# A graph network's softmax: each 128x128 transposition as two of 64 rows on the two row halves of TensorE

## The chip, the cores and the metric

The kernel runs on one core of one Trainium2 chip. The metric is device time in microseconds (us) of one execution, as the median of several runs. The engines are named as in the profile: PE is TensorE's matrix multiply, PEld its weight load, DVE is VectorE, ACT is ScalarE, POOL is GpSimd, SP is SyncE. PSUM is the accumulator memory that PE writes and that DVE and ACT read[...].

## What is computed

Four graph layers, each behind a layer norm and a ReLU, and each added to its input, on x of 32 batches, 512 nodes and 64 features, all in fp32. The last two have the softmax that the change touches:

```python
x = x + L0(h, adj, ...)          # h = relu(layernorm(x)), before each layer
x = x + L1(h, adj, ...)          # two rounds of adj @ h @ w, with relu
# layer 2: graph attention
Wh = h @ W.T; e = leaky_relu(Wh @ a1 [:, None] + Wh @ a2 [None, :], 0.2)
att = softmax(where(adj > 0, e, -9e15), axis=-1)
x = x + elu(att @ Wh)
# layer 3: eight heads, then an output layer, each of the form
def gat_layer(x, graph, W, b):
    h = x @ W
    s = (h @ h.T) * graph
    a = softmax(where(s == 0, -1e16, s), axis=2)
    return a @ h + b
```

## The kernel before, in words

The 512 nodes are four blocks of 128. Layers 0 and 1 come first, in four groups of eight batches, and are not touched. Layers 2 and 3 are done in *units*, each of which is two softmax problems of 512x512 side by side: `Gat` (layer 2: two batches, 16 units), `Heads` (layer 3: two heads of one batch, 128 units) and `Out` (the output layer: two batches, 16 units). After the 16 Gat units, eight Heads units and one Out unit alternate; the Out unit of a pair of batches stands behind the third Heads unit of the second batch after it. All are subclasses of `Pair`.

A unit takes four steps of each kind, and `run` (L609) interleaves the units by hand: in one turn of the loop at L618 it issues

- `scores(r)` of the current unit: two matmuls of 64 rows each, one for each problem, on the two row halves of PE (L472, s_ps, a tile of two banks, two such tiles);
- `transpose(j)` (L332) of the unit before, five turns late: for each of the two problems, the four 128x128 blocks of the probabilities p_att (L338) into one bank of the pool ps_m (pt_ps), and a copy of the bank to SBUF on ACT (L343, pt_att);
- with `transpose(1)`, `recips` (L355): the reciprocal of the softmax sums on DVE (L357, rec), eight small matmuls that spread it (L361, rec_ps), a copy (L369, recb);
- `values(j)`, a turn later: two matmuls av (L350) with the transposed probabilities;
- `end(j)`: the product with recb on DVE (L373, o_att), for Heads the head's output (L544, y_ps, and on ACT L549, cat), for Gat and Out the way back into x (L381);
- `prep(j)` for the next unit: for Heads the layer norm on DVE (L497 to L505, hn), a transposition with its copy (L178 and L180, hx) once in a batch, and g_ps (L516); for Out the accumulation gT_ps over all heads (L567, 16 matmuls over four turns), and gV_ps (L576);
- `soft(r)` of the current unit: for Heads and Out, DVE multiplies the scores by the graph (L461, s_att), makes the mask (L465, t_att) and takes the row maxima (L322, twice); ACT takes the exponential with its sum (L326, twice, p_att).

"First step" to "fourth step" below are these turns, counted by `scores(0)` to `scores(3)`. By the lags, rec_ps and g_ps lie in the third, y_ps in the fourth.

The pool ps_m has three banks, which serve pt_ps, rec_ps, g_ps, y_ps, gT_ps, gV_ps and the others; ps_s has two tiles of two banks, ps_v one bank for av. The engines run their own queues. The order in a queue follows the order of issue only roughly: the framework that builds the program moves instructions by its own estimate of when their inputs are ready. In the built program the reciprocal of L357 stands much earlier than the loop has it: mostly just behind the first s_att of the next unit, once the last L326 of its own unit is due. And the two L549 of a Heads unit stand between the two L326 of a fourth step.

Of the kernel before, what the change touches and what calls it, by code (L numbers as in the profile page):

```python
# [8 lines left out]
F32 = mybir.dt.float32  # L9
# [5 lines left out]
P = 128  # L15
# [7 lines left out]
def gnn_stack_kernel(  # L23
# [22 lines left out]
    nc = tc.nc  # L46
    B, N, F = x.shape
    C = N // P
# [59 lines left out]
    ident = const.tile([P, P], F32, name="ident")  # L108
# [12 lines left out]
    with tc.tile_pool(name="ps_setup", bufs=2, space=PSUM) as ps:  # L121
        for k in range(C):
            pt = ps.tile([P, N], F32, name="pt")
# [139 lines left out]
    ps_m = ctx.enter_context(tc.tile_pool(name="ps_m", bufs=3, space=PSUM))  # L263
# [13 lines left out]
    pt = ps_m.tile([P, H, F], F32, name="whT_ps", tag="m")  # L277
# [24 lines left out]
    def halves(k):  # L302
        return slice(k * F, (k + 1) * F)

    class Pair:
# [26 lines left out]
        def transpose(self, j):  # L332
            pt = pbuf.tile([P, 2, N], F32, name="pt_att", bufs=3)
            self.pts = getattr(self, "pts", []) + [pt]
            for k in range(2):
                ps = ps_m.tile([P, N], F32, name="pt_ps", tag="m")
                for r in range(C):
                    nc.tensor.transpose(  # L338
                        ps[:, r * P : (r + 1) * P],
                        self.p[:, k, r, j * P : (j + 1) * P],  # L340
                        ident,
                    )
                nc.scalar.copy(pt[:, k, :], ps)  # L343

        def values(self, j):
            pt = self.pts.pop(0)
# [339 lines left out]
```

## Time and profile before

| what | us |
|---|---|
| median of 3 runs (3112.18 to 3113.51) | 3113.04 |
| the profiled execution, its own time | 3115.21 |
| its span, first to last instruction | 3113.4 |
| PE busy in the span | 2842.9 |
| DVE busy | 2436.9 |
| ACT busy | 2005.0 |
| layers 0 and 1, about | 0 to 451 |
| Gat units, about | 465 to 800 |
| Heads and Out units, about | 766 to 3107 |

How to read it: a line of the timeline gives the start, the length, the engine, the line, the operation, the tiles out<-in, the shape and the count; what stands in brackets behind it is the idle time of the engine before it, and which instruction ended that. `64*128` behind a matmul is the rows and columns of PE that it uses. An fp32 matmul shows as two instructions, a transposition as one. Matmuls are pipelined, so that the start of one to the start of the next says more than their lengths. Times are from one profiled execution, which took 2.2 us more than the median of the runs.

### The profile page before, as it was taken

The numbers are of one execution on the slowest core, as the hardware profiler recorded it, in microseconds if no ns is written. First come the engines' busy times: TensorE is split into PE (matmuls) and PEld (weight loads), VectorE is DVE, ScalarE is ACT, GpSimd is POOL, SyncE is SP. The second block draws the span as 40 slices with busy tenths as digits, with TensorE's granted clock in tenths as the row PEclk, the third lists the DMA queues.
The fourth block names the chain that finished last, engine by engine and source line by source line (L and its number), as shares of the span: only waits on it lengthen the run. The fifth ranks groups of instructions, "written<-read, shape, count | busy, mean of one in ns | idle before, by whom it ended". The sixth has DMA issues, their size and how long they took to land.

```text
span 3113.4 us, 41619 instructions
## 1 busy us (share of the span) xinstructions
PE 2842.9 (91%) x15532; PEld 1380.7 (44%) x15532; DVE 2436.9 (78%) x4802; ACT 2005.0 (64%) x4586; POOL 99.1 (3%) x49
## 2 busy tenths in 40 slices
PE   4665658788999999999999999999999999999998
PEld 2333335444444444444444444444444444444443
DVE  5335348989988888979898988888898979898884
ACT  0110106766777777777777777777777777777775
POOL 3102100000000000000000000000000000000000
PEclk9887887998999999999999999999999999999999
DMA  3000000000000000000000000000000000000000
GB/s 80 0 0 0 0 1 1 1 1 1 1 1 5 1 4 1 4 1 4 1 4 1 4 4 1 4 1 4 1 4 1 4 1 4 1 5 4 1 4 4
DMA packets 9867, 13.09 MB, mean 4 GB/s; under 512 B 968, under 2 KB 9328, under 8 KB 9536
## 3 DMA queue, kind: packets, MB, share of 16 engines
q1 hardware_dynamic: 6832, 7.34, 0.7%
q8 instruction: 122, 2.00, 0.3%
q10 hardware_dynamic: 2080, 2.10, 0.2%
q0 software_dynamic: 752, 0.99, 0.2%
q14 instruction: 81, 0.66, 0.1%
HBM read 6.23 MB, written 4.19 MB: 3 GB/s over the span
## 4 chain that ended last, share of the span: by engine, by line
PE 82%; DVE 11%; ACT 4%; issue 1%; POOL 1%; DMA 0%; POOLq 0%; ACTq 0%; DVEq 0%
PE av L350 19%; PE pt_ps L338 18%; PE s_ps L472 17%; PE nt_ps L195 6%; PE rec_ps L361 5%; PE g_ps L516 4%; PE y_ps L544 4%; PE gT_ps L567 3%; PE po L206 2%; ACT p_att L326 2%; DVE s_att L461 1%; DVE l_att L432 1%; DVE mean L140 1%; DVE hn L164 1%; DVE t_att L322 1%
## 5 line engine op out<-in xcount | busy, mean ns | idle before, releaser
L326 ACT ACTIVATE p_att<-t_att,negmax 128x512 f32<-128x512 f32 x1152 | 825.2, 717 | 465.5 <-DVE negmax L322 465.4
L461 DVE TENSOR_TENSOR s_att<-s_ps,adj_p 128x1024 f32<-128x1024 f32 x576 | 703.4, 1222 | 225.3 <-PE s_ps L472 225.3
L338 PEld LDWEIGHTS pt_ps<-ident,p_att 128*128 128x128 f32 x5120 | 553.6, 141 | 509.5 <-ACT p_att L326 186.9
L322 DVE CUSTOM_DVE_ANT_0 t_att<-s_att,t_att 128x512 f32<-128x512 f32 x1152 | 752.4, 687 | 13.4
L343 ACT COPY pt_att<-pt_ps 128x512 f32<-128x512 f32 x1280 | 679.3, 581 | 119.1 <-PE pt_ps L338 118.8
L338 PE MATMUL pt_ps<-ident,p_att 128*128 128x128 f32 x5120 | 714.2, 282 | 28.5 <-DVE e L414 12.1
L472 PE MATMUL s_ps<-hx,g 64*128 64x512 f32 x2048 | 660.1, 624 | 2.0 <-DVE s_att L461 2.0
L350 PE MATMUL av<-pt_att,hn 128*64 128x512 f32 x2048 | 579.0, 611 | 0.0
L465 DVE TENSOR_SCALAR t_att<-s_att 128x1024 f32<-128x1024 f32 x576 | 393.1, 683 | 24.7 <-ACT pt_att L343 0.9
L472 PEld LDWEIGHTS s_ps<-hx,g 64*128 64x128 f32 x2048 | 204.3, 185 | 310.9 <-issue 121.4
L326 ACT ACTIVATION_READ_ACCUMULATOR p_att<-t_att,negmax 128x1 f32 x1152 | 216.1, 188 | 0.0
L361 PE MATMUL rec_ps<-ident,rec 128*64 128x128 f32 x2560 | 185.8, 283 | 22.3 <-ACT p_att L326 19.7
L195 PE MATMUL nt_ps<-adj_t,hn 128*128 128x512 f32 x256 | 135.0, 669 | 60.5 <-DVE hn L168 60.5
L199 ACT COPY nt<-nt_ps 128x512 f32<-128x512 f32 x48 | 28.1, 586 | 237.8 <-PE nt_ps L195 237.8
L361 PEld LDWEIGHTS rec_ps<-ident,rec 128*64 128x64 f32 x2560 | 144.0, 139 | 56.2 <-issue 26.4
L549 ACT ACTIVATE cat<-y_ps,bh 128x512 f32<-128x512 f32 x256 | 159.7, 673 | 4.4 <-PE y_ps L544 4.4
L350 PEld LDWEIGHTS av<-pt_att,hn 128*64 128x64 f32 x2048 | 115.6, 135 | 76.7 <-issue 76.4
L544 PE MATMUL y_ps<-o_att,wh_sb 64*128 64x512 f32 x512 | 145.6, 641 | 1.6 <-ACT pt_att L343 0.8
L516 PE MATMUL g_ps<-hx,m 64*128 64x512 f32 x256 | 143.7, 641 | 1.1 <-ACT pt_att L343 1.0
L246 DVE SCALAR_TENSOR_TENSOR x<-po,x 128x256 f32<-128x256 f32 x32 | 12.1, 419 | 167.5 <-PE po L206 167.5
L567 PE MATMUL gT_ps<-cat,wo_sb 128*64 128x512 f32 x512 | 131.4, 595 | 0.0
L373 DVE TENSOR_TENSOR o_att<-av,recb 128x512 f32<-128x512 f32 x160 | 108.9, 681 | 23.1 <-PE av L350 21.9
(117 smaller groups left out, 2118.5 us busy)
## 6 DMA issues: line engine op xcount, KB each, us to landing
out_dram<-x SPq DMA_DIRECT2D x32, 128.0 KB, 1.8
x<-in_x_dram ACTq DMA_DIRECT2D x2, 1024.0 KB, 19.0
x<-in_x_dram SPq DMA_DIRECT2D x2, 1024.0 KB, 19.0
adj_raw<-in_adj_dram SPq DMA_DIRECT2D x1, 1024.0 KB, 5.7
wh_sb<-in_L_gnn_Wh_dram POOLq DMA_DIRECT2D x2, 256.0 KB, 8.0
wo_sb<-in_L_gnn_W_out_dram POOLq DMA_DIRECT2D x1, 256.0 KB, 8.7
wl<-in_L_gnn_net_params_dram POOLq DMA_DIRECT2D x4, 16.0 KB, 8.0
bias_b<-in_L_gnn_bias_dram POOLq DMA_DIRECT2D x1, 32.0 KB, 7.7
```

What stands on the lines that cost most here:

```text
L195: nc.tensor.matmul(p, lhsT=lhs(k), rhs=adj_t[:, k, :], start=(k == 0), stop=(k == C - 1))
L322: nc.vector.tensor_tensor_reduce(out=ns[k], in0=s[k], in1=t[k], scale=-1.0, scalar=BIG, op0=OP.add, op1=OP.min, accum_out=self.negmax[:, k ...
L326: nc.scalar.activation(self.p[:, k, r, :], ns[k], AF.Exp, bias=self.negmax[:, k, r : r + 1], scale=-1.0, accum_out=self.sum[:, k, r : r + 1],)
L338: nc.tensor.transpose(ps[:, r * P : (r + 1) * P], self.p[:, k, r, j * P : (j + 1) * P], ident,)
L343: nc.scalar.copy(pt[:, k, :], ps)
L350: nc.tensor.matmul(self.av[halves(k), :], lhsT=self.v(k, j), rhs=pt[:, k, :], start=(j == 0), stop=(j == C - 1),)
L361: nc.tensor.matmul(ps[halves(k), r * P : (r + 1) * P], lhsT=rec[:, k, r : r + 1].to_broadcast([P, F]), rhs=ident, start=True, stop=True,)
L461: nc.vector.tensor_tensor(s, ps, adj_f[:, r, None, :].to_broadcast([P, 2, N]), OP.mult)
L465: nc.vector.tensor_scalar(t, s, 0.0, FLOW_NEG, op0=OP.is_equal, op1=OP.mult)
L472: nc.tensor.matmul(u.s_ps[:, k], lhsT=g[halves(k), r * P : (r + 1) * P], rhs=x[halves(k), :], start=True, stop=True,)
L516: nc.tensor.matmul(ps, lhsT=m2[rows, 2 * i : 2 * i + 2, :].rearrange("p h f -> p (h f)"), rhs=self.x[rows, :], start=True, stop=True,)
L544: nc.tensor.matmul(ps, lhsT=wh_sb[halves(k), h, :], rhs=self.o[halves(k), :], start=True, stop=True,)
```

## The change

The two problems' eight blocks are transposed as sixteen: each 128x128 block of p_att is split into its upper and lower 64 rows, and each half is transposed on its own row half of PE, with the matching 64x64 part of the identity. The two halves alternate. All the upper halves go to one bank and all the lower halves to another, so that a bank now holds both problems instead of one. The two copies on ACT each take a bank and write it into the two problems' rows of pt_att, in runs of 64 elements. Both banks are asked for at the start.

```diff
         def transpose(self, j):
             pt = pbuf.tile([P, 2, N], F32, name="pt_att", bufs=3)
             self.pts = getattr(self, "pts", []) + [pt]
+
+            ps = [ps_m.tile([P, 2, C, F], F32, name="pt_ps", tag="m") for half in range(2)]
             for k in range(2):
-                ps = ps_m.tile([P, N], F32, name="pt_ps", tag="m")
                 for r in range(C):
-                    nc.tensor.transpose(
-                        ps[:, r * P : (r + 1) * P],
-                        self.p[:, k, r, j * P : (j + 1) * P],
-                        ident,
-                    )
-                nc.scalar.copy(pt[:, k, :], ps)
+                    for half in range(2):
+                        nc.tensor.transpose(
+                            ps[half][:, k, r],
+                            self.p[halves(half), k, r, j * P : (j + 1) * P],
+                            ident[halves(half), halves(half)],
+                        )
+            pth = pt.rearrange("p k (r half q) -> p k r half q", r=C, half=2)
+            for half in range(2):
+                nc.scalar.copy(pth[:, :, :, half, :], ps[half])
```

## The prediction, as it was put on record

> **What bounds the kernel now.** First the totals, then the stage that holds three quarters of the span, then the chain of waits, then a stretch of the timeline. The first line below is the page's busy time of each engine; the second a window over the stage with the head and output units (its columns: length, then PE, PEld, DVE, ACT, POOL busy with instruction counts, granted clock); the third the chain that ended last.
>
> ```profile
> PE 2842.9 (91%) x15532; PEld 1380.7 (44%) x15532; DVE 2436.9 (78%) x4802; ACT 2005.0 (64%) x4586; POOL 99.1 (3%) x49
> ```
>
> ```profile
> 800.00:3080.00 2280.00, 2271.13 (x12858) 1061.18 (x12855) 1935.09 (x3807) 1719.06 (x3963) 4.57 (x2) 1.00 0.01 3
> ```
>
> ```profile
> PE 82%; DVE 11%; ACT 4%; issue 1%; POOL 1%; DMA 0%; POOLq 0%; ACTq 0%; DVEq 0%
> ```
>
> In that stage PE has 9 us free of 2280; DVE is busy 85%, ACT 75%. The timeline of PE in one step (start, length, line, count):
>
> ```profile
> 2049.01 1.09 PE L338 MATMUL pt_ps<-ident,p_att 128*128 128x128 f32 x8
> 2050.04 1.08 PE L350 MATMUL av<-pt_att,hn 128*64 128x512 f32 x4
> 2051.05 1.13 PE L472 MATMUL s_ps<-hx,g 64*128 64x512 f32 x4
> 2052.11 1.09 PE L338 MATMUL pt_ps<-ident,p_att 128*128 128x128 f32 x8
> ```
>
> Start to start: transposes 1.02 us, av 1.01, s_ps 1.06, together 3.09 with no gap. A plain unit (four steps; the third adds rec_ps and g_ps, the fourth y_ps) runs from s_att at 2049.13 to the same point at 2064.08: 14.95 us. So PE sets the pace. But DVE stands close behind, and its order matters. DVE at the end of one unit and through the next:
>
> ```profile
> 2047.25 0.69 DVE L322 CUSTOM_DVE_ANT_0 t_att<-s_att,t_att 128x512 f32<-128x512 f32 x1
> 2047.86 0.69 DVE L322 CUSTOM_DVE_ANT_0 t_att<-s_att,t_att 128x512 f32<-128x512 f32 x1
> 2049.13 1.23 DVE L461 TENSOR_TENSOR s_att<-s_ps,adj_p 128x1024 f32<-128x1024 f32 x1 [0.57 <-PE s_ps L472]
> 2050.68 0.20 DVE L357 RECIPROCAL rec<-sum_att 128x8 f32<-128x8 f32 x1 [0.32 <-ACT p_att L326]
> 2052.71 1.22 DVE L461 TENSOR_TENSOR s_att<-s_ps,adj_p 128x1024 f32<-128x1024 f32 x1
> 2056.39 1.22 DVE L461 TENSOR_TENSOR s_att<-s_ps,adj_p 128x1024 f32<-128x1024 f32 x1
> 2060.12 1.22 DVE L461 TENSOR_TENSOR s_att<-s_ps,adj_p 128x1024 f32<-128x1024 f32 x1 [0.43 <-PE s_ps L472]
> ```
>
> DVE is idle 0.57+0.32+0.43 = 1.32 us in this unit. The reciprocal needs the sum that ACT makes last, and ACT puts two activations of the head output between its last two exponentials:
>
> ```profile
> 2047.98 0.72 ACT L326 ACTIVATE p_att<-t_att,negmax 128x512 f32<-128x512 f32 x1 [0.86 <-DVE negmax L322]
> 2048.70 1.25 ACT L549 ACTIVATE cat<-y_ps,bh 128x512 f32<-128x512 f32 x2
> 2049.84 0.72 ACT L326 ACTIVATE p_att<-t_att,negmax 128x512 f32<-128x512 f32 x1
> 2050.45 0.19 ACT L326 ACTIVATION_READ_ACCUMULATOR p_att<-t_att,negmax 128x1 f32 x1
> ```
>
> Exponential to reciprocal: 2047.98 to 2050.68, 2.70 us, whatever PE does. Today s_att stands ahead of the reciprocal on DVE and covers most of it. Once per nine units it doesn't (the unit ahead of an output unit), and there the trace shows the naked wait:
>
> ```profile
> 2097.72 0.69 DVE L322 CUSTOM_DVE_ANT_0 t_att<-s_att,t_att 128x512 f32<-128x512 f32 x1
> ...
> 2100.54 0.20 DVE L357 RECIPROCAL rec<-sum_att 128x8 f32<-128x8 f32 x1 [2.12 <-ACT p_att L326]
> 2102.80 1.22 DVE L461 TENSOR_TENSOR s_att<-s_ps,adj_p 128x1024 f32<-128x1024 f32 x1 [2.06 <-PE s_ps L472]
> ```
>
> Here the 2.12 us cost nothing: PE was later still.
>
> **What the Trainium skill says.** "TensorE: Matmul & The Clock Gate", Part 3: matmuls on different row groups run side by side, and the loads of weights overlap. The trace agrees: four s_ps matmuls on alternating row halves take 1.13 us, each 0.59 or more; one 512-column stream on the whole array takes 0.41 (eight nt_ps in 3.44: (3.44-0.59)/7), so four in a row would need 1.8. "TensorEngine Tiling (Array Packing)", Gotcha 1: row tiles must write different banks, which the two tiles of the change do; Key Properties: a change of tiling mode drains the array. The trace agrees: s_ps costs 1.06 between other modes and 0.96 behind y_ps, of its own mode. "PSUM — Partial Sum Buffer", Engine vs sequencer instructions: VectorE and ScalarE are strict FIFO, so what stands behind a waiting reciprocal waits too; the row at 2100.54 agrees.
>
> **The transposes on PE.** 5120 of 128x128 become 10240 of 64x128, 16 per call instead of 8. The trace has such an instruction: whT_ps, eight in a row on one row half, 64 columns each. Two answers of the timeline, cut 0.1 us apart:
>
> ```profile
> 451.32 0.37 PE L279 MATMUL whT_ps<-ident,wh_sb 64*128 64x64 f32 x3 [0.89 <-PE po L206]
> 451.32 0.49 PE L279 MATMUL whT_ps<-ident,wh_sb 64*128 64x64 f32 x5 [0.89 <-PE po L206]
> ```
>
> Two more take 0.12: 0.06 each, against 0.12 for a whole one ((1.09-0.28)/7, 282 ns being the mean of one). If the halves run in pairs, a call is 7 x 0.06 plus about 0.18 to the next mode: 0.60 instead of 1.02. If they run one after the other, 16 x 0.06 is 1.0 and nothing is gained. I take pairs, since s_ps shows them. s_ps and the transposes are then of one mode: 0.10 less. Together 0.52 per call, 2.08 per unit: PE needs 12.9 instead of 14.95.
>
> **The copies.** Still two per call of 512 elements (581 ns each); they read a bank in one run and write runs of 64. No row shows ACT writing so; 0 is taken, up to 20 ns more (below zero excluded: same elements). They can begin only when the whole call is done, 0.6 us after its start instead of 0.5 for the first: nothing, as ACT waits on DVE.
>
> **The two banks at once.** Three banks serve all small results. A call now needs two of them at its start, the second about 0.44 us earlier than today. In plain units the banks come free by the copies of the step before, ahead of need. While an output unit's gT_ps holds one, the call waits for both copies; counted below.
>
> **What moves on DVE.** The instruction order of the two built programs differs there. In the program before, 126 of 160 reciprocals stand behind the s_att of the next unit and 16 (the units with gT_ps) ahead of it. In the changed one, 18 stand behind it and 124 ahead, directly behind the second L322 of the fourth step: 7 units of 9 have changed sides. The ACT order (exponential, two cat, exponential) stays, and so does PE's. Behind the waiting reciprocal stand s_att and all of the next unit's softmax. So DVE's loop in a plain unit is: steps without idle, 3.21 (in the unit before: s_att at 2041.44, the last L322 at 2044.04, and 0.61 from one L322 to what follows), 3.68 (2052.71 to 2056.39, with o_att), 3.21 and 3.21, plus rec 0.12, plus the naked wait 2.12: 15.6 us. One more term: g_ps in the third step needs the bank whose copy ACT makes after the second step's exponentials. In the trace that copy ends 5.2 us after the second s_att (57.32+0.53 against 52.71), and the fourth step's s_att starts 2.02 after g_ps (58.10 to 60.12): 7.2 against DVE's own 3.68+3.21 = 6.9. That adds 0.3: 15.95, 1.0 more than today.
>
> **The sum**, per cycle of nine units (eight head, one output; 16 cycles):
> - seven units with cat and the moved reciprocal: 7 x 1.0 = +7.0;
> - two of them carry hn and hx: today 0.59 each on PE; then DVE pays 0.61 for the hx copy and 0.7 for hn, of which 0.3 lies in the g_ps wait: 2 x (1.0-0.59) = +0.8;
> - the unit whose fourth step has no cat keeps its reciprocal behind s_att, and loses DVE's idle: -0.4;
> - the unit with gT_ps is PE's own (23.77 from 2079.03 to 2102.80): four calls x 0.52 = 2.1, and PE enters it some 0.9 further ahead of DVE than today (the naked wait just before gives it the time), less 0.3 for banks: -2.7 (bounds -1.5 and -5).
>
> +4.7 per cycle, +75 in all. The layers before the units are untouched; the first 16 units (490 to 800) are held by DVE (277 of 310 busy) and keep their reciprocal's place: 0, bounds -15 and +10. Against the profiled execution, 3115.2 us (span 3113.4), that is 3190; the median of the runs lies 2 below it, so **3188**.
>
> **Rivals.**
> - *PE's gain comes through.* If the moved reciprocal doesn't stop DVE (its sum comes early, or the wait falls where DVE is idle anyway), a plain unit falls to DVE's 13.3 and small waits, 14.0: 8 x 0.95 + 2.7, less 1.4 for hn and hx, 9 per cycle, 2970. For it: PE is 99.6% busy now. Against: DVE is FIFO, and the 2.12 is measured. It turns at 1.3 us: if the wait is shorter than DVE's idle of today, the change is faster.
> - *The halves don't pair.* Calls stay at 1.0; the plain units don't notice (PE 14.95 is under 15.95), the gT units lose their gain: +2.7 x 16 = +43, 3230.
> - *PE cools.* PE would idle about a fifth of the time. Between 490 and 800, where PE is busy 83%, the granted clock is 0.91; if it fell so here, the gT units and g_ps stretch: some 5% of PE's 2200 us, 3300.
> - *Gains and losses cancel.* The gT unit gains 5 instead of 2.7, the g_ps wait is hidden: 4.7-2.3-2.1 = 0.3 per cycle, 3118.
>
> **How the numbers follow.** The likeliest 0.55 (its own range 3150 to 3230), PE's gain 0.13, no pairing 0.13, cooling 0.07, cancelling 0.12. About 0.2% is what a measurement of this kernel can tell from no change. Faster: 0.13 and 0.03 of the cancelling case; same: 0.05; slower: the rest, 0.79. The range from 3110 to 3265 leaves out PE's gain and most of the cooling.
>
> **What would show it.** Right: the reciprocal's idle before it grows from 71 us in total to 200 or more, released by p_att L326; s_att waits for s_ps almost only in gT units; a call of 16 takes about 0.6 us; PE's share of the chain falls and DVE's and ACT's rise. Wrong: a call still takes 1.0 (no pairing), a clock under 0.98 after 800 us (cooling), or DVE over 92% busy there with little idle before the reciprocal (the gain came through).

## The result and the profile after

The changed kernel takes 3201.45 us (median of 4 runs, 3199.8 to 3202.94), the kernel before beside it 3113.28 us (3112.18 to 3115.0): a ratio of 1.028, 95% interval 1.0265 to 1.030. The execution profiled has a span of 3200.1 us. Code lines from L345 on stand four lower than before: L340 are the transpositions, L347 the copies, L361 the reciprocal, L465 s_att, L476 s_ps, L520 g_ps, L548 y_ps, L553 cat. In the runs further down the same instructions stand at other lines again; go by the names of the tiles.

First the page's busy times of the changed kernel, then the window over the Heads and Out units, then the chain that ended last:

```profile
PE 2642.8 (83%) x20652; PEld 1339.2 (42%) x20652; DVE 2432.6 (76%) x4802; ACT 2002.8 (63%) x4586; POOL 99.0 (3%) x49
```

```profile
800.00:3080.00 2280.00, 2007.75 (x16775) 985.40 (x16775) 1875.31 (x3697) 1659.05 (x3833) 4.57 (x2) 1.00 0.01 3
```

```profile
DVE 48%; PE 27%; ACT 20%; issue 4%; POOL 1%; DMA 0%; POOLq 0%; DVEq 0%; ACTq 0%
```

PE lost 200 us of work. In the window it was busy 2271 of 2280 us, and now is 2008; its share of the chain fell from 82% to 27%. But no engine took its place: DVE is busy 1875 us in the window, less than the 1935 of before. When the bound engine gets faster, the time gets longer and every engine is busy for less of it, the chain must run through waits from one engine to another. PE's granted clock is 1.00 as before, so it did not cool.

Four groups of the page of the changed kernel (line, tiles, count; busy us, mean ns; idle time before them and who ended it):

```profile
L465 DVE TENSOR_TENSOR s_att<-s_ps,adj_p 128x1024 f32<-128x1024 f32 x576 | 697.6, 1211 | 114.8 <-PE s_ps L476 114.7
...
L347 ACT COPY pt_att<-pt_ps 128x512 f32<-128x512 f32 x1280 | 679.8, 580 | 89.2 <-PE pt_ps L340 87.8
...
L520 PE MATMUL g_ps<-hx,m 64*128 64x512 f32 x256 | 143.7, 641 | 139.7 <-ACT pt_att L347 139.7
L361 DVE RECIPROCAL rec<-sum_att 128x8 f32<-128x8 f32 x160 | 32.2, 201 | 266.8 <-ACT p_att L326 266.8
```

Before, s_att waited 225 us for s_ps and the reciprocal 71 us for the last exponential. Now s_att waits 115, the reciprocal 267: DVE waits for ACT more than for PE. The timeline of DVE through a plain unit of the changed kernel, from one reciprocal to the next:

```profile
2067.44 0.20 DVE L361 RECIPROCAL rec<-sum_att 128x8 f32<-128x8 f32 x1 [2.12 <-ACT p_att L326]
2067.56 1.17 DVE L465 TENSOR_TENSOR s_att<-s_ps,adj_p 128x1024 f32<-128x1024 f32 x1
...
2070.72 1.22 DVE L465 TENSOR_TENSOR s_att<-s_ps,adj_p 128x1024 f32<-128x1024 f32 x1
...
2074.41 1.22 DVE L465 TENSOR_TENSOR s_att<-s_ps,adj_p 128x1024 f32<-128x1024 f32 x1
...
2077.98 1.22 DVE L465 TENSOR_TENSOR s_att<-s_ps,adj_p 128x1024 f32<-128x1024 f32 x1 [0.27 <-PE s_ps L476]
...
2083.47 0.20 DVE L361 RECIPROCAL rec<-sum_att 128x8 f32<-128x8 f32 x1 [2.12 <-ACT p_att L326]
2083.59 1.17 DVE L465 TENSOR_TENSOR s_att<-s_ps,adj_p 128x1024 f32<-128x1024 f32 x1
```

16.03 us from one s_att at the head of a unit to the next, against 14.95 before. And PE in one step of the changed kernel:

```profile
2144.74 1.13 PE L476 MATMUL s_ps<-hx,g 64*128 64x512 f32 x4
2145.70 0.66 PE L340 MATMUL pt_ps<-ident,p_att 64*128 64x64 f32 x16
2146.30 1.08 PE L354 MATMUL av<-pt_att,hn 128*64 128x512 f32 x4
```

The call of sixteen halves takes 0.60 us to the next start, against 1.02 for eight whole ones, and s_ps 0.96 against 1.06. The change does on PE what it says.

For what follows, the starts of s_att (four to a unit) cut the trace into units. The lengths of the nine units of a cycle, as medians over ten cycles (us), for both kernels and for the five experiments that the argument needs:

| unit | before | after | run 2 | run 1 | run 3 | run 9 | run 12 |
|---|---|---|---|---|---|---|---|
| 1, ahead of gT, with hn | 14.95 | 16.28 | 16.29 | 15.18 | 14.73 | 14.65 | 14.16 |
| 2, with gT_ps | 23.77 | 21.13 | 22.04 | 22.89 | 22.90 | 22.29 | 22.52 |
| 3, the Out unit | 14.94 | 16.08 | 16.60 | 14.16 | 14.24 | 14.23 | 13.75 |
| 4, with hx | 15.54 | 16.63 | 16.64 | 15.36 | 15.04 | 14.83 | 14.34 |
| 5, no cat at its end | 14.28 | 13.71 | 13.71 | 14.38 | 13.94 | 13.83 | 13.47 |
| 6, with hn and back_ps | 15.35 | 16.93 | 17.02 | 15.17 | 15.25 | 15.24 | 14.75 |
| 7, plain | 14.95 | 16.02 | 16.03 | 14.61 | 14.24 | 14.24 | 13.75 |
| 8, with hx | 15.54 | 16.64 | 16.64 | 15.37 | 15.04 | 14.83 | 14.34 |
| 9, plain | 14.95 | 16.02 | 16.03 | 14.79 | 14.33 | 14.23 | 13.75 |
| sum (16 cycles) | 144.3 | 149.5 | 151.0 | 141.9 | 139.7 | 138.4 | 134.8 |
| first s_att of a Heads unit, at | 765.8 | 767.2 | 758.4 | 764.2 | 765.6 | 765.1 | 765.0 |

### The profile page after: what moved, and what is told of

Read it like the earlier page. It is cut to its first block, busy times and chain, and to the rows that moved or that the text cites. A ratio compares the mean times of both kernels' runs of the same rounds, so it can differ in the third digit from the quotient of the medians.

```text
span 3200.1 us, 51783 instructions
## 1 busy us (share of the span) xinstructions
PE 2642.8 (83%) x20652; PEld 1339.2 (42%) x20652; DVE 2432.6 (76%) x4802; ACT 2002.8 (63%) x4586; POOL 99.0 (3%) x49
## 3 DMA queue, kind: packets, MB, share of 16 engines
q8 instruction: 161, 2.64, 0.4%
## 4 chain that ended last, share of the span: by engine, by line
DVE 48%; PE 27%; ACT 20%; issue 4%; POOL 1%; DMA 0%; POOLq 0%; DVEq 0%; ACTq 0%
DVE s_att L465 15%; DVE t_att L322 12%; ACT p_att L326 12%; DVE t_att L469 9%; PE nt_ps L195 6%; PE s_ps L476 4%; ACT cat L553 4%; PE g_ps L520 3%; PE av L354 3%; PE gT_ps L571 3%; DVE o_att L377 2%; ACT pt_att L347 2%; PE po L206 2%; PE pt_ps L340 2%; DVE hn L164 1%
## 5 line engine op out<-in xcount | busy, mean ns | idle before, releaser
L465 DVE TENSOR_TENSOR s_att<-s_ps,adj_p 128x1024 f32<-128x1024 f32 x576 | 697.6, 1211 | 114.8 <-PE s_ps L476 114.7
L322 DVE CUSTOM_DVE_ANT_0 t_att<-s_att,t_att 128x512 f32<-128x512 f32 x1152 | 752.6, 687 | 13.5
L347 ACT COPY pt_att<-pt_ps 128x512 f32<-128x512 f32 x1280 | 679.8, 580 | 89.2 <-PE pt_ps L340 87.8
L340 PE MATMUL pt_ps<-ident,p_att 64*128 64x64 f32 x10240 | 588.2, 228 | 165.8 <-ACT pt_att L347 74.5
L340 PEld LDWEIGHTS pt_ps<-ident,p_att 64*128 64x128 f32 x10240 | 486.9, 139 | 551.0 <-issue 181.1
L476 PE MATMUL s_ps<-hx,g 64*128 64x512 f32 x2048 | 704.6, 625 | 6.5 <-DVE s_att L465 6.5
L476 PEld LDWEIGHTS s_ps<-hx,g 64*128 64x128 f32 x2048 | 240.8, 186 | 286.4 <-issue 73.2
L520 PE MATMUL g_ps<-hx,m 64*128 64x512 f32 x256 | 143.7, 641 | 139.7 <-ACT pt_att L347 139.7
L361 DVE RECIPROCAL rec<-sum_att 128x8 f32<-128x8 f32 x160 | 32.2, 201 | 266.8 <-ACT p_att L326 266.8
L548 PE MATMUL y_ps<-o_att,wh_sb 64*128 64x512 f32 x512 | 193.9, 643 | 0.9 <-DVE o_att L377 0.9
L553 ACT ACTIVATE cat<-y_ps,bh 128x512 f32<-128x512 f32 x256 | 159.8, 673 | 6.6 <-PE y_ps L548 6.6
L520 PEld LDWEIGHTS g_ps<-hx,m 64*128 64x128 f32 x256 | 37.7, 184 | 253.0 <-ACT pt_att L347 250.7
```

Of the source, the lines that this page charges most:

```text
L322: nc.vector.tensor_tensor_reduce(out=ns[k], in0=s[k], in1=t[k], scale=-1.0, scalar=BIG, op0=OP.add, op1=OP.min, accum_out=self.negmax[:, k ...
L340: nc.tensor.transpose(ps[half][:, k, r], self.p[halves(half), k, r, j * P : (j + 1) * P], ident[halves(half), halves(half)],)
L347: nc.scalar.copy(pth[:, :, :, half, :], ps[half])
L465: nc.vector.tensor_tensor(s, ps, adj_f[:, r, None, :].to_broadcast([P, 2, N]), OP.mult)
L476: nc.tensor.matmul(u.s_ps[:, k], lhsT=g[halves(k), r * P : (r + 1) * P], rhs=x[halves(k), :], start=True, stop=True,)
L520: nc.tensor.matmul(ps, lhsT=m2[rows, 2 * i : 2 * i + 2, :].rearrange("p h f -> p (h f)"), rhs=self.x[rows, :], start=True, stop=True,)
```

## The experiments

All of them change only the order on an engine, or the order of the halves. A line of order is given by

```python
def behind(later, earlier):     # later comes after earlier in its engine's queue; no wait is added
    tc.add_manual_dep(later.ins, earlier.ins.name,
        mybir.DependencyInfo(mybir.DependencyClass.NoSync, mybir.DependencyReason.DATA), reason="order")
```

`satt` lists the s_att instructions and `exps` the exponentials, in the order of issue. Times are medians against the kernel before on the same chip (3112.4 to 3113.1 us).

Theory A is the prediction's: the reciprocal, moved ahead of s_att, makes DVE wait for ACT with nothing beside it. Theory B is its rival: the two banks that a call now needs at once hold up g_ps and s_att. (A bank is what one of the kernel's PSUM tiles of 128x512 fp32 values takes; ps_m hands out three.)

### Runs 1 to 4: the reciprocal's place, with halves and without

Run 1 keeps the change and puts the reciprocal back behind the first s_att of the next unit:

```diff
-            nc.vector.reciprocal(rec, self.sum)
+            done = nc.vector.reciprocal(rec, self.sum)
+            behind(done, satt[-2])
```

> The halves stay as in the changed kernel; only the reciprocal stands again behind the first s_att of the next unit, where the kernel before has it. Theory A (the moved reciprocal, which waits 2.12 us and holds up s_att, is what costs): its idle falls to about 1.0 us per unit, since s_att and its 1.2 us lie in it; a plain unit 14.6 to 14.9 us instead of 16.03, PE's gain in the gT units stays: about 4.2 per cycle under the kernel before, 3046 us (3020 to 3090). Theory B (the two banks asked for at once, and the copies that end later, hold up g_ps and through it s_att): the order matters little, 3180 to 3200 us, and the plain unit stays at about 16.

Measured: 3082.2 us, ratio 0.990 (0.9885 to 0.9915). The plain unit is 14.61, as A has it, and the reciprocal waits 62 us in all instead of 267. B falls as the main cause. But 36 us of what A expected are missing, most of them in the gT unit: 22.89, not the 21.1 that the changed kernel has (1.8 x 16 = 28).

Run 2 has the kernel before, with the reciprocal alone moved to where the change has it (made at the end of its own unit, and s_att behind it):

```diff
+        def early(self):
+            self.rec = tiny.tile([P, 2, C], F32, name="rec")
+            self.done = nc.vector.reciprocal(self.rec, self.sum)
...
+                if r == 0 and last and len(satt) > n and not isinstance(units[max(u - 3, 0)], Out):
+                    behind(satt[-1], last.done)
```

> The kernel before, with whole 128x128 transpositions, and only the reciprocal moved ahead of the next unit's s_att, as it stands in the changed kernel. Theory A: the naked wait of about 2.1 us appears here too, in seven units of nine; a plain unit is at least 15.6 us, no gain in the gT units: 3185 to 3215 us. Theory B (banks and copies): no loss without the halves, 3110 to 3120 us.

Measured: 3213.1 us, ratio 1.032 (1.0305 to 1.034). Not one transposition is touched, and the kernel loses more than by the change. DVE's timeline in run 2, the head of one unit and of the next:

```profile
2021.47 0.20 DVE L366 RECIPROCAL rec<-sum_att 128x8 f32<-128x8 f32 x1 [2.12 <-ACT p_att L335]
2021.59 1.17 DVE L473 TENSOR_TENSOR s_att<-s_ps,adj_p 128x1024 f32<-128x1024 f32 x1
...
2032.61 1.23 DVE L473 TENSOR_TENSOR s_att<-s_ps,adj_p 128x1024 f32<-128x1024 f32 x1 [0.28 <-PE s_ps L484]
...
2038.11 0.20 DVE L366 RECIPROCAL rec<-sum_att 128x8 f32<-128x8 f32 x1 [2.12 <-ACT p_att L335]
2038.23 1.17 DVE L473 TENSOR_TENSOR s_att<-s_ps,adj_p 128x1024 f32<-128x1024 f32 x1
```

The same 2.12 us. The short wait of the fourth s_att for s_ps, 0.27 us in the changed kernel, stands here too, with whole blocks. The units' table shows the same lengths as after, up to 0.1 us, but for units 2 and 3. The loss is in the cycles: 6.7 x 16 = 107 us; the Gat units, whose reciprocals this run moves too, give 7 back.

Run 3 keeps the change and puts the reciprocal behind the second s_att, `behind(done, satt[-1])`; run 4 does that to the kernel before.

> The halves stay; the reciprocal stands behind the second s_att of the next unit, nearer to where its result is first needed (rec_ps in the third step). Theory A: the sum is then ready before DVE gets there, no naked wait, and a plain unit is DVE's own 13.3 plus small waits, 13.6 to 14.2: 2950 to 2995 us, the rival of the prediction in which PE's gain comes through. Theory B (banks and copies): g_ps still waits for its bank, a plain unit of about 15.5 or more, 3150 to 3200 us.

> The kernel before, whole transpositions, with the reciprocal behind the second s_att as in the third run. Theory A, in full: without the halves PE sets the pace (14.95 us per plain unit, PE busy 99% after 800 us), so DVE's relief gives nothing: 3105 to 3120 us, and what the third run gains is PE's time from the halves. If the gain came from the reciprocal's place alone, this run would be as fast as the third: below 3050 us.

Measured: 3046.0 us, ratio 0.979 (0.977 to 0.980), and 3114.3 us, ratio 1.0003 (0.999 to 1.001). Run 4 is as A expects: without the halves DVE's relief is worth nothing, since PE sets the pace. Run 3 is faster, but it misses A's 2950 to 2995. Its plain unit is 14.24 us where DVE needs 13.43. DVE's timeline of run 3, one unit:

```profile
2013.56 1.22 DVE L476 TENSOR_TENSOR s_att<-s_ps,adj_p 128x1024 f32<-128x1024 f32 x1
2014.70 0.19 DVE L370 RECIPROCAL rec<-sum_att 128x8 f32<-128x8 f32 x1
...
2020.81 1.23 DVE L476 TENSOR_TENSOR s_att<-s_ps,adj_p 128x1024 f32<-128x1024 f32 x1 [0.27 <-PE s_ps L487]
...
2024.51 1.22 DVE L476 TENSOR_TENSOR s_att<-s_ps,adj_p 128x1024 f32<-128x1024 f32 x1 [0.33 <-PE s_ps L487]
```

The reciprocal waits for nothing now. What is left are two waits for s_ps, though PE has time to spare. Runs 9 to 12 look for their cause.

The runs that vary only this and the two kernels give one table (us):

| reciprocal of the unit before | whole blocks | halves | halves give |
|---|---|---|---|
| ahead of s_att | 3213 (run 2) | 3201 (after) | -12 |
| behind the first s_att | 3113 (before) | 3082 (run 1) | -31 |
| behind the second s_att | 3114 (run 4) | 3046 (run 3) | -68 |

The halves help in every row. (In the first row about 9 us of their gain are hidden, since run 2 moves the reciprocals of the Gat units too and is faster there; in the cycles alone the halves give 24 us.) The change moved one place right and one row up.

### Run 5: what the naked wait is made of

The reciprocal is held ahead of s_att as in run 2; beside that only the two cat move behind the last exponential: `behind(cat, exps[-1])`.

> The changed kernel with its reciprocal ahead of s_att, and only the two cat activations put behind the second exponential of the fourth step instead of between the two. Theory A (the naked wait is 2.12 us because two cat of 0.57 each stand ahead of the last exponential): the reciprocal's wait falls to about 1.0 us, and with it the plain unit by up to 1.1 us from 16.03: 3075 to 3120 us. A part may come back: the next transposition needs the bank that the first cat empties, and that now ends about 0.7 us later; by the timeline of the third run, s_att could then start some 0.8 us behind the reciprocal and the plain unit be about 15.0. Rival (the wait is the latency of the exponential and its sum, whatever lies between): the wait stays at 2.1 and the time at 3195 to 3205 us.

Measured: 3110.6 us, ratio 0.9992 (0.9985 to 0.9998). The reciprocal's wait is 0.97 us in the timeline and the plain unit 15.01, both as expected. So the 2.12 us were 0.97 of exponential and sum, and two cat. Over a cycle this run takes 144.37 us, the kernel before 144.26: with a wait of 0.97 us the change just breaks even. That is a rough mark, since the later cat costs something of its own: the transpositions wait 133 us on PE for its bank from 800 to 3000 us, against 56 in the changed kernel. The Gat units, whose reciprocals this run moves too, are 8 us shorter (757.8 against 765.8), and about 4 come back behind the cycles measured.

### Runs 6 and 7: do the halves pair?

All upper halves first, then all lower ones, in run 6 on top of run 3, in run 7 on the changed kernel:

```diff
-            for k in range(2):
-                for r in range(C):
-                    for half in range(2):
+            for half in range(2):
+                for k in range(2):
+                    for r in range(C):
```

> The third run (3046 us) with one thing more: the upper halves of a call are all transposed first, then all the lower ones, instead of alternately. If the short call comes from pairs on the two row halves, a call goes from 0.58 back to about 1.0 us, PE sets the pace again with a plain unit of 14.5 to 15 us, and the time is 3090 to 3120 us. If a half costs less by itself, with or without a partner, the call stays at 0.6 and the time at 3040 to 3055 us.

> The changed kernel with the reciprocal where the change has it, and the halves in turn instead of alternately: the prediction's rival in which the halves don't pair. It put +43 us on that (gT units only). The trace of after and the second run (whole transpositions in the same order, 3213 us) say less: 22.04 against 21.13 us in the gT unit and nearly the same in the others. So 3205 to 3225 us by the runs, 3244 us by the prediction's term.

Measured: 3073.5 us, ratio 0.987 (0.986 to 0.989), and 3221.6 us, ratio 1.0345 (1.033 to 1.036). PE in run 6:

```profile
2005.58 1.13 PE L487 MATMUL s_ps<-hx,g 64*128 64x512 f32 x4
2006.54 0.96 PE L349 MATMUL pt_ps<-ident,p_att 64*128 64x64 f32 x16
2007.43 1.08 PE L363 MATMUL av<-pt_att,hn 128*64 128x512 f32 x4
```

In turn a call takes 0.89 us, alternately 0.59. Cut the timeline of PE inside one call, and the count shows how many halves have started by then. First the changed kernel, cut at 2145.80 and 2145.92, then run 6, cut at 2006.62, 2006.74 and 2006.98:

```profile
2145.70 0.29 PE L340 MATMUL pt_ps<-ident,p_att 64*128 64x64 f32 x4
2145.70 0.41 PE L340 MATMUL pt_ps<-ident,p_att 64*128 64x64 f32 x8
```

```profile
2006.54 0.28 PE L349 MATMUL pt_ps<-ident,p_att 64*128 64x64 f32 x2
2006.54 0.40 PE L349 MATMUL pt_ps<-ident,p_att 64*128 64x64 f32 x4
2006.54 0.65 PE L349 MATMUL pt_ps<-ident,p_att 64*128 64x64 f32 x11
```

Alternately, four more halves take 0.12 us: two start nearly together every 0.06 us, eight times in a call. In turn, two more take 0.12 us, each alone; then seven more take 0.25, because near the middle of the call three pairs form, presumably where the last upper and the first lower halves meet. The starts show these three pairs in 394 of the 395 calls of run 6 that ran through without a wait after 800 us. So the halves do pair, and a half alone costs the 0.06 us of whT_ps. (The two halves also write two banks; no run tells the row half from the bank.) Run 6 is no test of a call without any pair: it has 13 starts 0.06 us apart where 16 were expected. That is why its call is shorter than the 1.0 assumed, and why run 6 lies between what its two theories expect. With s_ps still at 0.96, PE is then no longer what holds a plain unit (14.23). Run 7 came out as the runs before it had let expect. Of run 6's 27 us over run 3, 16 are in the cycles (140.7 against 139.7), 12 in the units before them; of run 7's 20 over the changed kernel, 8 and 12. Why the first units lose 12 us by it was not tried.

### Run 8: one cat behind the last exponential

On top of run 3, the second cat of a unit is put behind the last exponential.

> The third run (halves alternately, reciprocal behind the second s_att, 3046 us) with the second cat of a unit put behind the last exponential; the first stays between the two, since its bank is the one that the next transposition waits for. Nothing waits for the second cat soon. If ACT's order at the end of a unit still costs anything, it shows in the gT unit, whose last step is a chain over ACT (exponential, two cat, exponential, gT copy: 7.75 us in every kernel so far): 0.6 us less there, and 3030 to 3040 us in all. If not, 3046 us as before.

Measured: 3046.0 us, ratio 0.9785 (0.977 to 0.980): nothing. The gT unit's last step stays at 7.75 us. The edit changed the order inside the chain and not its length: the gT copy still stands behind both cat and both exponentials.

### Runs 9 to 12: where the rest of PE's gain went

All four are run 3 with another order on ACT. Run 9 puts the cat ahead of the first exponential of the fourth step (`cats` holds the cat issued last, the second of the two):

```diff
+                if k == 0 and r == C - 1 and cats:
+                    behind(exps[-1], cats.pop())
```

> Where does the rest of PE's gain go? The third run (3046 us) is at 14.24 us in a plain unit, against 13.43 that DVE needs (3 x 3.21, 3.68 and 0.12). In its trace s_att waits about 0.4 us at the head of a unit: s_ps stands on PE behind a call of halves that waits for its second bank until the first cat is done, and ACT does that cat behind the first exponential of the fourth step. Here both cat stand ahead of that exponential. Theory C (the banks, of which a call needs two at once, take back a part of the gain): the fourth step loses 0.3 to 0.45 us in some seven units of nine, 2995 to 3015 us. Rival (s_ps is late for PE's own work): 3040 to 3050 us.

Measured: 3023.0 us, ratio 0.971 (0.970 to 0.973), between what the two theories expect. PE's waits from 800 to 3000 us, run 3 and then run 9 (us in all, times, longest):

```profile
PE g_ps L531 <- ACT pt_att L356: 72.2, 123, 1.2
PE pt_ps L349 <- ACT cat L564: 61.4, 111, 1.5
```

```profile
PE g_ps L535 <- ACT pt_att L360: 131.7, 124, 1.2
...
PE pt_ps L353 <- ACT cat L568: 1.2, 2, 0.7
```

The wait for cat is gone, and the wait of g_ps grew by as much. The plain unit stays at 14.24; the gain is mostly in the gT unit (22.90 to 22.29) and the two with hx. So the wait for cat was not what held the plain unit, and the expectation named the wrong bank for it.

Runs 10 and 11 put the second call's copies ahead of the second step's exponentials, without and with run 9's edit:

```diff
             for half in range(2):
-                nc.scalar.copy(pth[:, :, :, half, :], ps[half])
+                done = nc.scalar.copy(pth[:, :, :, half, :], ps[half])
+            if j == 1 and last[0] is not self:
+                behind(exps[-2], done)
```

> The third run (3046 us) with the two copies of the second call put ahead of the second step's exponentials on ACT, which in that trace is idle 1.3 us before them. g_ps waits for the bank that the first of these copies empties (0.49 us in a plain unit), and s_att of the fourth step for s_ps behind it (0.29 us). Theory C (banks): that wait goes, 0.3 us in the third step of six units of nine, 3010 to 3025 us. Rival: g_ps is late for another reason (hx, or PE's order), 3040 to 3050 us.

> Both edits to ACT's order on top of the third run. Theory C: both waits for banks go, and a plain unit comes down to about 13.5 us, DVE's own time: 2960 to 2990 us, near the 2970 of the rival in which PE's gain comes through. If the two waits stand in for each other, it is no better than the better of the two runs before.

Measured: 3056.0 us, ratio 0.982 (0.980 to 0.983), and 3043.8 us, ratio 0.978 (0.976 to 0.979). Both are slower than what they build on. ACT in run 10 shows that the edit missed its aim:

```profile
2009.61 0.72 ACT L338 ACTIVATE p_att<-t_att,negmax 128x512 f32<-128x512 f32 x1 [1.91 <-DVE negmax L334]
...
2010.33 1.05 ACT L362 COPY pt_att<-pt_ps 128x512 f32<-128x512 f32 x2
2011.28 0.73 ACT L338 ACTIVATE p_att<-t_att,negmax 128x512 f32<-128x512 f32 x1
```

The step's other exponential went ahead of the copies, after ACT had been idle for 1.91 us. g_ps still waited (78 us in all from 800 to 3000 us), and ACT was late for the fourth step, which went from 3.70 to 4.05 us. Run 12 names both, on top of run 11:

```diff
                 behind(exps[-2], done)
+                behind(exps[-1], done)
```

> In the two runs before, only one of the second step's two exponentials stood behind the copies: the trace shows the other one still ahead of them (exponential, two copies, exponential), so that g_ps still waited, 78 and 122 us in all. Here both stand behind the copies, and the two cat ahead of the fourth step's first exponential as in the ninth run (3023 us), where g_ps waits 1.03 us in a plain unit and s_att behind it 0.27 in the third and, by PE's later start, 0.32 in the fourth step. Theory C (the bank for g_ps is what is left): g_ps starts right behind av, both waits of s_att go, a plain unit takes 13.5 to 13.7 instead of 14.24 us, in six units of nine: 2955 to 2985 us. Rival (PE's own work or DVE's order makes s_ps late): 3015 to 3030 us.

Measured: 2969.0 us, ratio 0.954 (0.952 to 0.9555). PE in run 12, third step, and the window over its Heads and Out units:

```profile
2041.51 1.03 PE L372 MATMUL av<-pt_att,gV 128*64 128x512 f32 x4
2042.47 0.69 PE L540 MATMUL g_ps<-hx,m 64*128 64x512 f32 x1
```

```profile
800.00:2900.00 2100.00, 2067.26 (x17132) 1017.38 (x17130) 1902.90 (x3780) 1689.61 (x3919) 4.57 (x2) 1.00 0.01 3
```

g_ps starts 0.96 us behind av, without a wait; the wait of s_att in the third step is gone, and the plain unit is 13.75, a little above the 13.5 to 13.7 expected. What its last 0.3 us over DVE's 13.43 are was not tried. PE is busy 98% again. So Theory C holds with g_ps's bank as its place: the order in which ACT empties the three banks held back PE's gain.

That a call takes two of them at once is not shown to be the reason. The wait of g_ps is there without the halves; run 2, PE from 800 to 3000 us:

```profile
PE g_ps L528 <- ACT pt_att L352: 89.0, 87, 1.1
```

Only the wait for cat comes with the halves: 56 us on PE in the changed kernel and 61 in run 3, none in the kernel before and in run 2. The two banks can explain that one, but no run gives the halves their banks one after the other. The kernel before was not tried with run 12's order on ACT.

## Why the prediction came out as it did, step by step

The forecast was 3188 us by +4.7 us per cycle; the measured difference is 88 us, of which the cycles show 5.2 x 16 = 83.

- **PE's call.** Forecast 0.60 us, 0.10 less for s_ps; measured 0.59 and 0.10, and in the way that was forecast: eight pairs, each as long as the one half of whT_ps. The price read from whT_ps held.
- **The copies.** Taken as 0; 580 ns against 581.
- **The moved reciprocal.** Right, and shown: the 2.12 us stand in the timeline, run 2 has the loss without the change, runs 1 and 3 have the change without the loss. Forecast +1.0 per plain unit, measured +1.07. The closeness is in part luck: the forecast's terms add up to 15.85 us (15.55 and 0.3) and not to the 15.95 written, which would have been +4.0 per cycle and 3177 us; and the fourth step, 5.45 us by these terms (3.21, 0.12 and 2.12), took 5.61. That VectorE is a strict FIFO (the Trainium skill, "PSUM — Partial Sum Buffer", Engine vs sequencer instructions) is what makes one short reciprocal hold up a whole unit; in the trace s_att starts 0.12 us behind it each time. (The row at 2100.54 that the prediction named for this can't show it, since the s_att behind it waited for PE anyway.) Why the framework moved it isn't shown by any run.
- **hn and hx.** The sum was right (+0.8; measured excess over plain units +0.9), the place wrong: the units with hx lose no more than plain ones (+1.09, +1.10), those with hn do (+1.33, +1.58).
- **The unit without cat at its end.** -0.4 forecast, -0.57 measured.
- **The gT unit.** -2.7 forecast, -2.64 measured: luck, out of two wrong sizes. Forecast were 2.1 from four shorter calls, 0.9 from PE's lead, and 0.3 back for banks. Run 2, with whole blocks, has -1.73 from the lead alone: the step ahead of the unit lasts so long by the naked wait that PE is ahead when the unit starts (its first step 3.16 us instead of 4.84). The calls then give 0.91, in the second and third steps only. The last step is 7.75 us with and without halves: it is a chain from DVE over exponential, two cat, exponential, gT copy and gV_ps to s_ps, where PE waits. Where the naked wait goes, as in runs 1 and 3, the lead goes with it; that is what their expectations overlooked.
- **The two banks.** Forecast as nothing in plain units, and in the changed kernel that is right: the wait behind g_ps, forecast as 0.3 us by ACT's order and measured at 0.27, stands in run 2 with whole blocks too, and the wait for cat, which the halves add, lies under the naked wait. Once that cover is gone the banks cost: without the wait for cat run 3 is 23 us faster (run 9), and without both waits 77 us, 0.49 us in a plain unit (run 12).
- **The first units.** 0 forecast, +1.4 measured.
- **The signs.** Those named in advance came: 267 us of the reciprocal's idle time, calls of 0.6 us, a chain with less of PE and more of DVE and ACT, and of s_att's 115 us of waits for s_ps about 83 in the gT units and right behind them.

**The rivals.** *PE's gain comes through* was put at 2970 with a turning point of 1.3 us. The point is nearer 1.0 (roughly, by run 5): of DVE's idle of 1.32 before, the waits behind g_ps don't go. And 2970 is what run 12 reaches, but only with the orders of DVE and of ACT both mended; moving the reciprocal out of the way alone gives 3046. *The halves don't pair* was put at 3230 by calls of 1.0 us in the gT unit; run 7 has 3222, by calls of 0.89 and 12 us in the first units that the rival didn't have; with three pairs left in each call it is not the rival in full. *PE cools*: the clock is 1.00 from 800 us on, and 0.91 between 490 and 800 as before. *Gains and losses cancel* wanted more from the gT unit and a hidden g_ps wait; neither came.

## What to carry to other kernels

When an edit goes through a scheduler, compare the order of the instructions on every engine before costing the edit itself: here the order cost 107 us in the cycles and the edit gave 24 of them back; with the reciprocal's place put right the same edit gained 67 us on the kernel before, and with ACT's order mended too the kernel came out 144 us ahead of it. A short instruction that waits at the head of a FIFO costs its wait, not its length, so look for the place in the queue where its input is long ready. And a gain on the bound engine is worth only what the next wait lets through; after each wait that goes, look at which one grew, as g_ps's did in run 9.

## What was not expected of the hardware

- Two transpositions of 64 rows that start together on the two row halves take 0.06 us, as long as one of them alone, against 0.11 for a whole block (medians from start to start after 800 us: a pair 62 ns in the changed kernel, a half alone 62 in run 6, a whole block 109 in the kernel before). By these figures two halves one behind the other would cost 0.12, so the gain is all in the pairs. Together with s_ps, which is then of the same mode, a call costs PE 0.53 us less than one of whole blocks (0.43 and 0.10).
- Order alone doesn't keep the halves apart: with all upper ones first, three pairs still form in a call (run 6), which takes 0.89 us.
- ACT writes runs of 64 fp32 values as fast as one run of 512: 580 and 581 ns.
- PE's clock stays at 1.00 with PE busy 88% of the stage.
